# Shared expert of a post-norm transformer block in blocks of 512 tokens for its last six of eight, with a PSUM bank for each half of a chunk

## The chip, the cores and the metric

The kernel runs on one core of a Trainium2 chip. The metric is the device time of one execution in microseconds (us). A core has five engines with instruction queues of their own: PE (TensorE, matrix products; its weight loads are listed apart as PEld), DVE (VectorE), ACT (ScalarE), POOL (GpSimd) and SP (SyncE, which here only issues DMAs). They meet through semaphores. Matmul results go to PSUM, eight banks of 128 partitions x 512 fp32 numbers; everything else lives in SBUF.

## What is computed

The input is x, [2, 1024, 512] in fp32, taken as 2048 tokens of 512 numbers. Attention with low-rank updates on q, k, v and o comes first, then a residual and a layer norm; its result is called x1. The second half is a mixture of experts on x1 with a shared expert beside it, a residual and a last layer norm. That half, cut:

```python
xt = x.reshape(T, d)                                  # T = 2048, d = 512
probs = jax.nn.softmax(xt @ Wg, axis=-1)              # E = 8 experts
eidx = jnp.argmax(probs, axis=-1)
gate = jnp.take_along_axis(probs, eidx[:, None], 1)[:, 0]
pos = ...                                             # running count of tokens per expert
keep = pos < C                                        # C = 256 places per expert
flat = jnp.where(keep, eidx * C + pos, E * C)
xd = zeros(E * C, d).at[flat].set(xt, mode='drop').reshape(E, C, d)
h = silu(einsum('ecd,edh->ech', xd, W1)) * einsum('ecd,edh->ech', xd, W3)   # H = 704
oe = einsum('ech,ehd->ecd', h, W2)
out = take(oe, flat) * (gate * keep)
shared = silu(xt @ sw1) * (xt @ sw3) @ sw2
return out + shared
```

## The kernel before

**Precision.** Every fp32 operand of a large matmul is split into a high part, rounded to TensorE's fp32r type, and a low part that holds the rest. A product is three matmuls: high by high, high by low, low by high. So x1 transposed is held twice (`xth`, `xtl`), a weight chunk holds both parts (`w13s`, `w2s`), and so does a hidden activation (`hs`).

**Stages.** Projections, attention, the output projection (`op`, L744) with the first layer norm, the shared expert (first product at 631.76 us), and then the eight experts one after the other. x1 stays in SBUF in two tiles, `x1a` and `x1b`, eight rows of 128 tokens each, with a gate and a token number behind every row.

**The shared expert** (loop at L1121) goes through eight blocks of 256 tokens. The hidden size of 704 is cut into six chunks of 128, of which the last is 64. For each chunk:
- `ffn1` (L881, matmuls at L890): one PSUM bank `h`, its first 256 columns for W1, the others for W3, 12 matmuls of 256 columns each (four slices of d by three products). A matmul has a 128 x 128 weight as its stationary operand and streams `xth` or `xtl` of the 256 tokens. Chunk 5 has W1 and W3 side by side in one stationary operand and takes 12.
- `glu` (L898): silu on ACT into `sl` (L901), product on DVE in PSUM (L902).
- `split_h` (L907): high part of the hidden activation on ACT (L910), low part on DVE (L916); for chunk 5 on half of the partitions, with one more ACT copy.

`shared_out` (L1049) follows for the block before, called after chunk 1 (`pend()`, L1128): for each half of 128 tokens `ffn2` (L919, matmuls at L934) makes 17 matmuls of 512 columns into a bank `y`, with the hidden activation as the stationary operand; DVE adds the residual into `bt`, and SP stores it to `bs_d` in DRAM.

PSUM has three banks `hp` for h, two `tp` for transposes and small products, two `y`. `hs` has eight buffers, and the transposed token blocks have five (`XTB`).

**What runs between.** A table `SCHED` (L84) says after which (block, chunk) the small operations are issued: `p` transposes a block of tokens (`prep_block`, L537; `xpose`, L461), `a` and `b` make router logits for 256 tokens (`logits_a`, L511: eight matmuls of 256 columns; `logits_b`, L525), `q` and `m` finish the first layer norm. `r` steps through the router (L940), a generator with two stops: `r0` runs up to the prefix sum over tokens per expert, `r1` to the prefix sum of the dropped tokens, `r2` to its end, where the slot of every token is known (`slot_i`, L1035), and POOL scatters 16 rows of 128 tokens to `xd_d` in DRAM with indirect DMAs (L1038). `r0` stands at block 3, chunk 3, `r1` at block 3, chunk 5, `r2` at block 4, chunk 1.

TensorE's order is that of the code. For the other engines the framework's scheduler decides the order within the shared expert; in the expert loop it is that of the code for them too.

**What is fetched for the experts.** `w13_load` (L545; its DMA is at L554) loads a 512 KB chunk of an expert's W1 and W3 over rows of x1 in turn, seven places; the scatters of those rows must be through before. It runs `AHEAD` = 5 chunks ahead of use. `w13_split` (L571) makes the high part on ACT (L562) and the low part on DVE; the six splits of expert 0 are issued in the last block. After block 5 SP is told to read `meta` (gates and token numbers, L1142) and the rows of expert 0 (`load_rows`, L1068, DMA at L1072), which wait for all scatters (`reads_xd`, L1057), and four chunks of W2. `prep_expert(0)` (L1075) transposes these rows (`tpe`, L464) after chunk 3 of the last block. The last `shared_out` runs in expert 0, after its chunk 1.

**The experts** (loop at L1152) use the same `ffn1` and `ffn2` with 256 rows each, so 256 columns to a matmul; this part is the same in both kernels but for one call.

Of the kernel before, what the change touches and what calls it, by code (L numbers as in the profile page):

```python
# [9 lines left out]
F32 = mybir.dt.float32  # L10
# [8 lines left out]
P = 128  # L19
# [5 lines left out]
KC = D // P  # L25
# [30 lines left out]
REC = 5  # L56
NRM = 0
K_AT = 6
XTB = 5


ADDS = {
# [16 lines left out]
OPROJ1 = 0  # L79
NRM_DVE = (NU - 3, NU - 2)  # L80
ROOT_LAG, NORM_LAG = 1, 4
HSB = 8
TAIL = (
    "l0 l1 t0 s0 s1 n1 n2 w0 o1 o2 r0 s2 o3 p0 r1 m0 s3 o4 r2 m1 o5 p1 a0 s4 r3 m2 o6 r4 m3 "  # L84
    "s5 o7 r5 m4"
).split()
SCHED = {
# [4 lines left out]
}  # L92
W13 = 5 * 1024 + 512
W2W = 6 * 512
# [4 lines left out]
def kernel(  # L99
# [5 lines left out]
    def f(ap):  # L105
        return ap.bitcast(F32)
# [331 lines left out]
                prep_w(3, load_w(3))  # L438
            xs = xn

    po, rt, xts = {}, {}, {}
    turn3 = cycle(range(4))
    NB = T // 256

# [7 lines left out]
            return one.tile([P, 512], F32, name=nm, tag="one")  # L452
        return po["ps"].tile([P, 512], F32, name=nm, tag=tag, bufs=bufs)

    def new_xt(nm):
        return (
            po['flx'].tile([P, KC, 256], F32R, name=f"xth{nm}", tag="xth", bufs=XTB),
            po['flx'].tile([P, KC, 256], F32R, name=f"xtl{nm}", tag="xtl", bufs=XTB),
        )

    def xpose(xt, half, row, nm):  # L461
        tp = bank(f"tp{nm}_{half}", "tp", 2)
# [72 lines left out]
        )  # L535

    def prep_block(blk):  # L537
        xts[blk] = new_xt(f"s{blk}")
        for hf in range(2):
            i = blk * 2 + hf  # L540
            xpose(xts[blk], hf, x1[i // 8][:, i % 8, 0:D], f"s{blk}")
# [3 lines left out]
    def w13_load(e, c):  # L545
        w = 512 if c == 5 else 1024
        if e < 0:
            raw = po["frw"].tile([P, 2, 512], F32, name=f"w13r{c}", tag="w13r", bufs=RB)
        else:
            n = (e * 6 + c) % 7  # L550
            raw = x1[n // 4][:, n % 4 * 2 : n % 4 * 2 + 2, 0:D]
        raw = raw[:, : w // 512, :]
        src = s13 if e < 0 else w13[e]
        sp.dma_start(  # L554
            out=raw, in_=src[:, c * 1024 : c * 1024 + w].rearrange("p (a b) -> p a b", b=512)
        )
        wraw[e, c] = raw
# [13 lines left out]
    def w13_split(e, c):  # L571
        w13_high(e, c)
        w13_low(e, c)
# [285 lines left out]
    def w2_load(e, c):  # L859
        if e < 0:  # L860
            raw = fr.tile([P, 512], F32, name=f"w2r{c}", tag="bt", bufs=BTB)
        elif e == E - 1:
            n = (E * 6 + c) % 7
            raw = x1[n // 4][:, n % 4 * 2, 0:D]
        else:
            raw = fr.tile([P, 512], F32, name=f"w2r{e}_{c}", tag="w2r", bufs=4)
        src = s2 if e < 0 else w2[e]
        sp.dma_start(out=raw, in_=src[:, c * 512 : c * 512 + 512])
        wraw[e, 6 + c] = raw
# [9 lines left out]
        wchunk[e, 6 + c] = hl  # L879

    def ffn1(e, blk, xt, c):  # L881
        hp = bank(f"h{e}_{blk}_{c}", "hp", 3)
        wt = wchunk[e, c]
        nw = 1 if c == 5 else 2
        for j in range(nw):
            n = 0
            for k in range(KC):
                ws = [wt[:, q, (k * nw + j) * P : (k * nw + j) * P + P] for q in range(2)]
                for lhs, rhs in ((ws[0], xt[0]), (ws[0], xt[1]), (ws[1], xt[0])):
                    pe.matmul(  # L890
                        hp[:, j * 256 : j * 256 + 256], lhs, rhs[:, k, :],
                        start=n == 0, stop=n == 11,
                    )
                    n += 1
        return hp


    def glu(e, blk, c, hp):  # L898
        sl = fr.tile([P, 256], F32, name=f"sl{e}_{blk}_{c}", tag="sl", bufs=2)
        if c < 5:  # L900
            act.activation(sl, hp[:, 0:256], AF.Silu)  # L901
            dve.tensor_tensor(hp[:, 256:512], hp[:, 256:512], sl, ALU.mult)  # L902
        else:
            act.activation(sl[64:128], hp[0:64, 0:256], AF.Silu)
            dve.tensor_tensor(hp[64:128, 0:256], hp[64:128, 0:256], sl[64:128], ALU.mult)

    def split_h(e, blk, c, hp):  # L907
        hs = fr.tile([P, 2, 256], F32R, name=f"hs{e}_{blk}_{c}", tag="hs", bufs=HSB)
        if c < 5:
            act.copy(hs[:, 0, :], hp[:, 256:512])  # L910
            dve.tensor_tensor(hs[:, 1, :], hp[:, 256:512], f(hs[:, 0, :]), ALU.subtract)
        else:
            pr = hp[64:128, 0:256]
            act.copy(hs[64:128, 1, :], pr)
            act.copy(hs[0:64, 0, :], pr)
            dve.tensor_tensor(hs[64:128, 0, :], pr, f(hs[64:128, 1, :]), ALU.subtract)  # L916
        return hs
# [128 lines left out]
            tc.add_to_no_dep_group("xd", sc_)  # L1046
            scatters.append(sc_)

    def shared_out(blk, hss):  # L1049
        for hf in range(2):  # L1050
            i = blk * 2 + hf
            o = ffn2(-1, blk, hss, hf)
            bt = fr.tile([P, D], F32, name=f"bt{i}", tag="bt", bufs=BTB)
            dve.tensor_tensor(bt, o, x1[i // 8][:, i % 8, 0:D], ALU.add)
            sp.dma_start(out=bs_d[i * P : i * P + P, :], in_=bt)
# [17 lines left out]
            xrows[e, hf] = xd  # L1073

    def prep_expert(e):  # L1075
        xte[e] = new_xt(f"e{e}")
        for hf in range(2):
            xpose(xte[e], hf, xrows[e, hf], f"e{e}")

# [38 lines left out]
    for at, ops in SCHED.items():  # L1118
        sched[at] = [(stage[op[0]], int(op[1])) for op in ops.split()]
    pend = None  # L1120
    for st in range(NB):  # L1121
        hss = []
        for c in range(6):
            hp = ffn1(-1, st, xts[st], c)
            glu(-1, st, c, hp)
            hss.append(split_h(-1, st, c, hp))
            if c == 1 and pend:
                pend()  # L1128
            for fn, a_ in sched.get((st, c), ()):
                fn(a_)  # L1130
            n = (st - NB + 1) * 6 + c
            if 0 <= n + AHEAD < E * 6:
                w13_load(*divmod(n + AHEAD, 6))
            if st == NB - 1:
                if c == 0:
                    load_rows(1)
                if c == 3:
                    prep_expert(0)
                w13_split(0, c)
        if st == NB - 3:  # L1140
            reads_xd(
                sp.dma_start(  # L1142
                    out=meta, in_=xd_d[:, D : D + 2].rearrange("(j p) c -> p j c", p=P)
                )
            )
            load_rows(0)
            for q in range(4):
                w2_load(0, q)
        pend = lambda st=st, hss=hss: shared_out(st, hss)

    with tc.manual_schedule(engines=MAN4):
        last = None  # L1152
        for e in range(E):
            nxt = e + 1
            hss = []
            for c in range(6):
# [13 lines left out]
                if nxt < E:  # L1170
                    if c == 0 and nxt + 1 < E:
                        load_rows(nxt + 1)
                    w13_high(nxt, c)
                hss.append(split_h(e, 0, c, hp))
                if nxt < E:
                    w13_low(nxt, c)
                if c == 1:
                    if e:
                        for hf in range(2):
                            expert_out(e - 1, last, hf)  # L1180
                    else:
                        pend()
                if c == 3 and nxt < E:
                    prep_expert(nxt)
                if e in (0, E - 1) and c in (3, 5):
# [90 lines left out]
```

## Time and profile before

| | |
|---|---|
| median of 10 runs | 1061.19 us (1060.38 to 1063.26) |
| the profiled execution's own time | 1059.73 us |
| its span in the profile | 1058.0 us |
| PE busy | 1034.0 us, 98% |
| DVE, ACT, POOL busy | 686.9, 527.2, 573.5 us |
| the eight experts' FFN1 matmuls (L890, 256 columns), mean of one | 704 of 283 ns and 352 of 285 ns |
| FFN2 matmuls (L934, 512 columns) from `hs`, mean of one | 260 of 390 ns |
| bytes moved by DMA | 151.93 MB, mean 144 GB/s |

The profile is that of one execution, taken by the hardware; its span runs from the first instruction to the last, and the execution's own time has 1.73 us more around it. The page gives, for each engine, busy time and instructions; the span in 40 equal slices (26.45 us each) with the busy share of each engine in tenths, the clock that TensorE was granted (PEclk), and what the DMA engines moved; and groups of equal instructions, each with its line in the code, its output and input, and the mean time of one. Matmuls overlap, so the time of one is longer than the distance from one start to the next. The timeline lists single instructions with their start; in brackets stands how long the engine was idle before and what ended that ("issue": nothing that the profile shows; "remote": a semaphore from elsewhere). A table by windows gives busy time per engine in a chosen stretch.

### The profile page before, as it was taken

What the parts mean: (1) busy time and instruction counts of PE and PEld (TensorE: products, weight loads), DVE (VectorE), ACT (ScalarE), POOL (GpSimd) and SP (SyncE); (2) the same over time, 40 slices, a digit from 0 to 9 for tenths busy, and PEclk for the clock granted to TensorE, in tenths of its full rate; (3) what the DMA queues carried; (4) which work ended last, traced back from release to release, by engine and by line L of the source; (5) the groups of instructions that cost most, each with busy time, mean ns of one, the idle gap of its engine ahead of it and who ended that gap; (6) DMA issues with size and microseconds to landing.
All of it is one profiled execution on the core that took longest, in us unless ns stands there. A gap on an engine that the chain in (4) does not pass through costs nothing. (4 is left out here: it accounts for less than half of the span.)

```text
span 1058.0 us, 16557 instructions
## 1 busy us (share of the span) xinstructions
PE 1034.0 (98%) x5994; PEld 745.2 (70%) x5994; DVE 686.9 (65%) x1192; ACT 527.2 (50%) x1023; POOL 573.5 (54%) x406
## 2 busy tenths in 40 slices
PE   9999999999999999999999999999979999999995
PEld 7888774444444455544444389999969999999994
DVE  7732788788888877778887873324412557777752
ACT  5422216666666645566666635223112447555552
POOL 4000006999999986979995263000320046766674
PEclk9999999999999999999999999999989999999998
DMA  8866863464646553635649441000370456777721
GB/s 293 284 219 213 254 195 91 91 136 109 134 94 147 121 115 83 138 82 125 146 103 188 92 120 52 20 21 20 119 221 31 130 179 228 254 246 243 258 86 59
DMA packets 86025, 151.93 MB, mean 144 GB/s; under 512 B 15492, under 2 KB 24196, under 8 KB 85944
## 3 DMA queue, kind: packets, MB, share of 16 engines
q1 hardware_dynamic: 76344, 117.31, 37.8%
q0 software_dynamic: 9600, 33.58, 13.4%
q8 instruction: 47, 0.77, 0.3%
q14 instruction: 34, 0.28, 0.1%
HBM read 95.83 MB, written 33.78 MB: 123 GB/s over the span
## 5 line engine op out<-in xcount | busy, mean ns | idle before, releaser
L197 DVE TENSOR_REDUCE mt<-s 128x1 f32<-128x512 f32 x512 | 324.0, 682 | 79.0 <-PE s L189 78.6
L659 POOL TENSOR_TENSOR pt<-pt,pt 128x1024 f32<-128x1024 f32 x138 | 336.7, 2943 | 0.1
L629 ACT ACTIVATE pt<-st 128x512 f32<-128x512 f32 x512 | 269.1, 601 | 131.5 <-PE st L620 111.6
L620 PE MATMUL st<-qs,ks 98*128 98x512 f32 x512 | 213.1, 427 | 1.3 <-DVE x1a L347 0.7
L189 PE MATMUL s<-ks,qs 96*128 96x512 f32 x512 | 200.1, 398 | 1.0 <-DVE mt L197 1.0
L620 PEld LDWEIGHTS st<-qs,ks 98*128 98x128 f32 x512 | 95.6, 188 | 133.2 <-issue 93.1
L656 POOL DMA_DIRECT2D pt<-pt x40 | 37.3, 1122 | 187.0 <-PE st L620 163.9
L890 PE MATMUL h<-xthe,w13s 128*128 128x256 f32 x704 | 129.9, 283 | 0.0
L878 POOL TENSOR_TENSOR w2s<-w2r,w2s 128x512 fp32r<-128x512 f32 x42 | 65.9, 1590 | 104.8 <-ACT w2s L877 104.6
L189 PEld LDWEIGHTS s<-ks,qs 96*128 96x128 f32 x512 | 97.0, 189 | 20.4 <-DVE mt L197 5.7
L890 PEld LDWEIGHTS h<-xthe,w13s 128*128 128x128 f32 x704 | 110.7, 191 | 0.3
L890 PE MATMUL h<-xtle,w13s 128*128 128x256 f32 x352 | 100.2, 285 | 0.1
L639 PE MATMUL av<-pt,vt 128*32 128x512 f32 x512 | 75.3, 605 | 0.0
L639 PE MATMUL av<-pt,x1b 128*32 128x512 f32 x512 | 68.2, 605 | 0.0
L890 PEld LDWEIGHTS h<-xtle,w13s 128*128 128x128 f32 x352 | 67.4, 191 | 1.0 <-DVE xtle L468 0.3
L1038 POOL DMA_INDIRECT xd_d<-x1a,slot_i x8 | 7.9, 987 | 110.5 <-DVE slot_i L1035 108.3
L934 PE MATMUL y<-w2s,hs 128*128 128x512 f32 x260 | 60.9, 390 | 0.0
L934 PEld LDWEIGHTS y<-w2s,hs 128*128 128x128 f32 x260 | 48.2, 188 | 10.2 <-DVE hs L916 0.5
L331 ACT ACTIVATE oh<-o,bqk_sb 128x512 fp32r<-128x512 f32 x32 | 22.0, 689 | 57.9 <-PE o L316 54.6
L901 ACT ACTIVATE sl<-h 128x256 f32<-128x256 f32 x40 | 15.5, 386 | 60.4 <-PE h L890 59.1
L316 PE MATMUL o<-xh,wh 128*128 128x512 f32 x116 | 45.3, 391 | 0.1
L316 PE MATMUL o<-xl,wh 128*128 128x512 f32 x116 | 45.3, 390 | 0.0
(830 smaller groups left out, 1842.4 us busy)
## 6 DMA issues: line engine op xcount, KB each, us to landing
pt<-pt POOLq DMA_DIRECT2D x40, 512.0 KB
x1a<-in_w_dram SPq DMA_DIRECT2D x24, 512.0 KB
w2r<-in_w_dram SPq DMA_DIRECT2D x42, 256.0 KB
qkd<-oh SPq DMA_DIRECT2D x32, 256.0 KB
qkd<-ol SPq DMA_DIRECT2D x32, 256.0 KB
x1b<-in_w_dram SPq DMA_DIRECT2D x16, 512.0 KB
qs<-qkd SPq DMA_DIRECT2D x30, 256.0 KB
ks<-qkd SPq DMA_DIRECT2D x18, 256.0 KB
```

The lines of the kernel that those rows point to most:

```text
L189: pe.matmul(s1, Qs[u % 3][0:96, h, qt * P : qt * P + P], Ks[g % 2][0:96, h, kh * 512 : kh * 512 + 512], start=True, stop=True,)
L197: dve.tensor_reduce(mts[u][:, c, kh : kh + 1], s1, AX.X, ALU.max)
L316: pe.matmul(o, lhs, rhs, start=k + i == 0, stop=k + i == KC + 1)
L331: act.activation(oh, o, AF.Identity, bias=bias)
L620: pe.matmul(sb, Ks[g % 2][:, h, kc * P : kc * P + P], Qs[u % 3][:, h, :], start=True, stop=True,)
L629: act.activation(pts[t, h // 2][:, h % 2, :], sb, AF.Exp, scale=SCALE)
L639: pe.matmul(avs[u][32 * h : 32 * h + 32, :], vts[g][:, kc, 32 * h : 32 * h + 32], pts[t, h // 2][:, h % 2, :], start=kc == 0, stop=kc == 7 ...
L656: pool.dma_start(out=pts[i + 1, pr], in_=pts[i, pr], accum_op=ALU.add)
L659: eng.tensor_tensor(accs[u, pr], accs[u, pr], pts[i, pr], ALU.add)
L878: pool.tensor_tensor(hl[:, 1, :], raw, f(hl[:, 0, :]), ALU.subtract)
L890: pe.matmul(hp[:, j * 256 : j * 256 + 256], lhs, rhs[:, k, :], start=n == 0, stop=n == 11,)
L934: pe.matmul(o, lhs, rhs, start=n == 0, stop=n == 16)
```

## The change

The eight blocks of 256 tokens become five: two of 256, then three of 512 (`BLOCKS`, pairs of first block and size). A wide block makes a chunk in two banks, one for W1 and one for W3, with 12 matmuls of 512 columns each (`ffn1_wide`), and the silu, product and split on 512 columns at once (`glu_wide`, `split_wide`). `hp` gets four banks. The transposed tokens lie in pairs of blocks, two buffers of 512 for five of 256; the hidden activations lie in pairs too, four buffers, and the first two chunks of a wide block in the buffers of the raw shared weights.

The four FFN2 halves of a wide block are issued after chunk 0 of the block behind it, and those of the last one in expert 0 after its first chunk. The table of small operations is new: `r0` after chunk 3 and `r1` after chunk 5 of the second wide block, `r2` after chunk 0 of the last one. The reads of `meta`, of expert 0's rows and the four W2 loads stand behind `r2` there. Loads and splits of expert 0's weights go by the same count of chunks, two for each wide one. Raw weights use six places in x1 instead of seven.

```diff
--- before.py
+++ after.py
...
 REC = 5
 NRM = 0
 K_AT = 6
-XTB = 5
+XTB = 2
 
 
 ADDS = {
...
 OPROJ1 = 0
 NRM_DVE = (NU - 3, NU - 2)
 ROOT_LAG, NORM_LAG = 1, 4
-HSB = 8
+HSB = 4
+
+BLOCKS = ((0, 1), (1, 1), (2, 2), (4, 2), (6, 2))
...
 SCHED = {
     (0, 0): "q6 m5", (0, 1): "p2 q7 m6", (0, 2): "a1 m7", (0, 3): "b0", (0, 4): "p3", (0, 5): "b1",
-    (1, 0): "a2 p4", (1, 1): "a3", (1, 2): "b2 a4", (1, 3): "b3 p5", (1, 4): "b4",
-    (1, 5): "p6", (2, 0): "a5", (2, 1): "b5 a6", (2, 3): "b6", (2, 5): "p7",
-    (3, 1): "a7", (3, 2): "b7", (3, 3): "r0", (3, 5): "r1", (4, 1): "r2",
+    (1, 0): "a2", (1, 1): "b2", (1, 2): "a3", (1, 3): "b3",
+    (2, 0): "p4", (2, 1): "a4 p5", (2, 2): "a5", (2, 3): "b4", (2, 4): "b5",
+    (3, 0): "p6", (3, 1): "a6 p7", (3, 2): "b6 a7", (3, 3): "b7 r0", (3, 5): "r1", (4, 0): "r2",
 }
 W13 = 5 * 1024 + 512
 W2W = 6 * 512
...
                 prep_w(3, load_w(3))
             xs = xn
 
-    po, rt, xts = {}, {}, {}
+    po, rt, xts, xts2 = {}, {}, {}, {}
     turn3 = cycle(range(4))
     NB = T // 256
 
...
             return one.tile([P, 512], F32, name=nm, tag="one")
         return po["ps"].tile([P, 512], F32, name=nm, tag=tag, bufs=bufs)
 
-    def new_xt(nm):
-        return (
-            po['flx'].tile([P, KC, 256], F32R, name=f"xth{nm}", tag="xth", bufs=XTB),
-            po['flx'].tile([P, KC, 256], F32R, name=f"xtl{nm}", tag="xtl", bufs=XTB),
-        )
+    pairs = {}
+
+
+    def new_xt(nm, i):
+        if i % 2 == 0:
+            pairs[nm] = [
+                po["flx"].tile([P, KC, 512], F32R, name=f"xt{q}{nm}{i}", tag=f"xt{q}", bufs=XTB)
+                for q in "hl"
+            ]
+        return [z[:, :, i % 2 * 256 : i % 2 * 256 + 256] for z in pairs[nm]]
 
     def xpose(xt, half, row, nm):
         tp = bank(f"tp{nm}_{half}", "tp", 2)
...
         )
 
     def prep_block(blk):
-        xts[blk] = new_xt(f"s{blk}")
+        xts[blk] = new_xt("s", blk)
+        if blk % 2:
+            xts2[blk - 1] = pairs["s"]
         for hf in range(2):
             i = blk * 2 + hf
             xpose(xts[blk], hf, x1[i // 8][:, i % 8, 0:D], f"s{blk}")
...
         if e < 0:
             raw = po["frw"].tile([P, 2, 512], F32, name=f"w13r{c}", tag="w13r", bufs=RB)
         else:
-            n = (e * 6 + c) % 7
+            n = (e * 6 + c) % 6
             raw = x1[n // 4][:, n % 4 * 2 : n % 4 * 2 + 2, 0:D]
         raw = raw[:, : w // 512, :]
         src = s13 if e < 0 else w13[e]
...
         wchunk[e, 6 + c] = hl
 
     def ffn1(e, blk, xt, c):
-        hp = bank(f"h{e}_{blk}_{c}", "hp", 3)
+        hp = bank(f"h{e}_{blk}_{c}", "hp", 4)
         wt = wchunk[e, c]
         nw = 1 if c == 5 else 2
         for j in range(nw):
...
         return hp
 
 
+    def ffn1_wide(blk, xt, c):
+        wt = wchunk[-1, c]
+        hps = []
+        for j in range(1 if c == 5 else 2):
+            hp = bank(f"h{blk}_{c}{j}", "hp", 4)
+            n, nw = 0, 1 if c == 5 else 2
+            for k in range(KC):
+                ws = [wt[:, q, (k * nw + j) * P : (k * nw + j) * P + P] for q in range(2)]
+                for lhs, rhs in ((ws[0], xt[0]), (ws[0], xt[1]), (ws[1], xt[0])):
+                    pe.matmul(hp, lhs, rhs[:, k, :], start=n == 0, stop=n == 11)
+                    n += 1
+            hps.append(hp)
+        return hps
+
+    def glu_wide(blk, c, hps):
+        sl = fr.tile([P, 512], F32, name=f"sl{blk}_{c}", tag="sl", bufs=2)
+        if c < 5:
+            act.activation(sl, hps[0], AF.Silu)
+            dve.tensor_tensor(hps[1], hps[1], sl, ALU.mult)
+        else:
+            act.activation(sl[64:128], hps[0][0:64], AF.Silu)
+            dve.tensor_tensor(hps[0][64:128], hps[0][64:128], sl[64:128], ALU.mult)
+
+
+    def split_wide(blk, c, hps):
+        if c < 2:
+            hs = po["frw"].tile([P, 2, 512], F32R, name=f"hw{blk}_{c}", tag="w13r", bufs=RB)
+        else:
+            hs = fr.tile([P, 2, 512], F32R, name=f"hw{blk}_{c}", tag="hw", bufs=HSB)
+        if c < 5:
+            act.copy(hs[:, 0, :], hps[1])
+            dve.tensor_tensor(hs[:, 1, :], hps[1], f(hs[:, 0, :]), ALU.subtract)
+        else:
+            pr = hps[0][64:128]
+            act.copy(hs[64:128, 1, :], pr)
+            act.copy(hs[0:64, 0, :], pr)
+            dve.tensor_tensor(hs[64:128, 0, :], pr, f(hs[64:128, 1, :]), ALU.subtract)
+        return hs
+
+
     def glu(e, blk, c, hp):
-        sl = fr.tile([P, 256], F32, name=f"sl{e}_{blk}_{c}", tag="sl", bufs=2)
+        sl = fr.tile([P, 512], F32, name=f"sl{e}_{blk}_{c}", tag="sl", bufs=2)[:, 0:256]
         if c < 5:
             act.activation(sl, hp[:, 0:256], AF.Silu)
             dve.tensor_tensor(hp[:, 256:512], hp[:, 256:512], sl, ALU.mult)
...
             tc.add_to_no_dep_group("xd", sc_)
             scatters.append(sc_)
 
-    def shared_out(blk, hss):
-        for hf in range(2):
+    def shared_out(blk, hss, n=2):
+        for hf in range(n):
             i = blk * 2 + hf
             o = ffn2(-1, blk, hss, hf)
             bt = fr.tile([P, D], F32, name=f"bt{i}", tag="bt", bufs=BTB)
...
             xrows[e, hf] = xd
 
     def prep_expert(e):
-        xte[e] = new_xt(f"e{e}")
+        xte[e] = new_xt("e", e)
         for hf in range(2):
             xpose(xte[e], hf, xrows[e, hf], f"e{e}")
 
...
     for at, ops in SCHED.items():
         sched[at] = [(stage[op[0]], int(op[1])) for op in ops.split()]
     pend = None
-    for st in range(NB):
+    for st, (blk, nb) in enumerate(BLOCKS):
         hss = []
         for c in range(6):
-            hp = ffn1(-1, st, xts[st], c)
-            glu(-1, st, c, hp)
-            hss.append(split_h(-1, st, c, hp))
-            if c == 1 and pend:
-                pend()
+            if nb == 1:
+                hp = ffn1(-1, blk, xts[blk], c)
+                glu(-1, blk, c, hp)
+                hss.append(split_h(-1, blk, c, hp))
+            else:
+                hps = ffn1_wide(blk, xts2[blk], c)
+                glu_wide(blk, c, hps)
             for fn, a_ in sched.get((st, c), ()):
                 fn(a_)
-            n = (st - NB + 1) * 6 + c
-            if 0 <= n + AHEAD < E * 6:
-                w13_load(*divmod(n + AHEAD, 6))
-            if st == NB - 1:
-                if c == 0:
-                    load_rows(1)
-                if c == 3:
-                    prep_expert(0)
-                w13_split(0, c)
-        if st == NB - 3:
-            reads_xd(
-                sp.dma_start(
-                    out=meta, in_=xd_d[:, D : D + 2].rearrange("(j p) c -> p j c", p=P)
+            if c == 0 and blk + nb == NB:
+                reads_xd(
+                    sp.dma_start(
+                        out=meta, in_=xd_d[:, D : D + 2].rearrange("(j p) c -> p j c", p=P)
+                    )
                 )
-            )
-            load_rows(0)
-            for q in range(4):
-                w2_load(0, q)
-        pend = lambda st=st, hss=hss: shared_out(st, hss)
+                load_rows(0)
+                for q in range(4):
+                    w2_load(0, q)
+            if c == 2 - nb and pend:
+                pend()
+            if nb == 2:
+                hss.append(split_wide(blk, c, hps))
+            for v in range(c * nb, c * nb + nb):
+                bv, cv = blk + v // 6, v % 6
+                n = (bv - NB + 1) * 6 + cv
+                if 0 <= n + AHEAD < E * 6:
+                    w13_load(*divmod(n + AHEAD, 6))
+                if bv == NB - 1:
+                    if cv == 0:
+                        load_rows(1)
+                    if cv == 3:
+                        prep_expert(0)
+                    w13_split(0, cv)
+        pend = lambda blk=blk, nb=nb, hss=hss: shared_out(blk, hss, 2 * nb)
 
     with tc.manual_schedule(engines=MAN4):
         last = None
...
                     if c == 0 and nxt + 1 < E:
                         load_rows(nxt + 1)
                     w13_high(nxt, c)
+                if e == 0 and c == 0:
+                    pend()
                 hss.append(split_h(e, 0, c, hp))
                 if nxt < E:
                     w13_low(nxt, c)
-                if c == 1:
-                    if e:
-                        for hf in range(2):
-                            expert_out(e - 1, last, hf)
-                    else:
-                        pend()
+                if c == 1 and e:
+                    for hf in range(2):
+                        expert_out(e - 1, last, hf)
                 if c == 3 and nxt < E:
                     prep_expert(nxt)
                 if e in (0, E - 1) and c in (3, 5):
```

Left out: the same change of 7 to 6 in `w2_load`, and in `glu` and `split_h` the cutting of the narrow block's tile out of a 512-wide one (`sl`, `hw`).

More of the change, by code (lines that the diff above doesn't have):

```diff
@@ L862, in w2_load @@
         elif e == E - 1:
-            n = (E * 6 + c) % 7
+            n = (E * 6 + c) % 6
             raw = x1[n // 4][:, n % 4 * 2, 0:D]
@@ L907, in split_h @@
     def split_h(e, blk, c, hp):
-        hs = fr.tile([P, 2, 256], F32R, name=f"hs{e}_{blk}_{c}", tag="hs", bufs=HSB)
+        if c % 2 == 0:
+            pairs["h"] = fr.tile([P, 2, 512], F32R, name=f"hs{e}_{blk}_{c}", tag="hw", bufs=HSB)
+        hs = pairs["h"][:, :, c % 2 * 256 : c % 2 * 256 + 256]
         if c < 5:
```

## The prediction, made before the changed kernel was run

> **What bounds the kernel now.** I read the page's busy list first, then the slices, then the pitch of the matmuls in the timeline, and last the one stretch in which TensorE isn't full.
>
> ```profile
> PE 1034.0 (98%) x5994; PEld 745.2 (70%) x5994; DVE 686.9 (65%) x1192; ACT 527.2 (50%) x1023; POOL 573.5 (54%) x406
> ...
> PE   9999999999999999999999999999979999999995
> ...
> PEclk9999999999999999999999999999989999999998
> ```
>
> TensorE is busy for 98% of the span and in every slice but one and the last; no other engine passes 65%. So the time goes with TensorE's work, and with the one dip in slice 30, where its granted clock dips too. The change works in the shared expert (631.76 to about 842.7 us), which holds that dip.
>
> The 283 and 390 ns that the page gives for a 256-wide and a 512-wide matmul are latencies of overlapping instructions. The price is the pitch, from start to start:
>
> ```profile
> 699.41 0.28 PE L890 MATMUL h-1_2_2_7228<-xths,w13s-1_2_6332 128*128 128x256 f32 x1
> ...
> 702.29 0.28 PE L890 MATMUL h-1_2_3_7259<-xths,w13s-1_3_6376 128*128 128x256 f32 x1
> ...
> 693.99 0.39 PE L934 MATMUL y-1_1_1_7192<-w2s-1_0_6527,hs-1_1_0_6816 128*128 128x512 f32 x1
> ...
> 697.39 0.39 PE L934 MATMUL y-1_1_1_7192<-w2s-1_5_6552,hs-1_1_5_7078 128*128 128x512 f32 x1
> ```
>
> The first pair is one chunk of FFN1 (first product), 24 matmuls: 2.88 us, 0.120 each, so 0.240 for 512 columns. The second pair is 15 matmuls of FFN2 (second product): 3.40 us, 0.2267 each. One wide costs 0.0133 less than two narrow ones.
>
> The dip, by windows (after the length: busy PE, PE loads, DVE, ACT, POOL, then granted clock, share of the DMA engines, GB/s):
>
> ```profile
> 757.00:759.00 2.00, 2.00 (x19) 2.00 (x18) 0.86 (x2) 0.40 (x2) 1.70 (x2) 1.00 0.64 251
> 761.00:763.00 2.00, 2.00 (x19) 2.00 (x19) 1.05 (x3) 1.08 (x3) 1.60 (x2) 1.00 0.98 207
> 767.00:769.00 2.00, 1.27 (x6) 0.76 (x5) 0.00 (x0) 0.00 (x0) 1.69 (x2) 1.00 0.97 376
> 771.00:773.00 2.00, 0.82 (x3) 0.19 (x1) 0.69 (x2) 0.37 (x1) 1.70 (x2) 0.74 1.00 390
> 773.00:775.00 2.00, 0.63 (x2) 0.57 (x2) 0.00 (x0) 0.00 (x0) 1.39 (x3) 0.50 1.01 268
> 777.00:779.00 2.00, 1.41 (x4) 1.02 (x4) 0.28 (x1) 0.38 (x1) 0.00 (x0) 0.50 0.68 261
> 779.00:781.00 2.00, 2.00 (x6) 1.53 (x5) 1.23 (x3) 0.37 (x1) 0.00 (x0) 0.50 0.02 6
> ```
>
> From 755.40 POOL issues 16 scatters of tokens (L1038), one each 1.27 us until 774.61. Alone they leave TensorE full (757 to 759). From 760.48 four 512 KB loads of expert 0's weights, each released by two scatters, fill the DMA engines. Some 5 us later TensorE starves, with no wait that the profile names ("issue" in the timeline), and ACT sees TensorE's ends late:
>
> ```profile
> 772.46 0.58 PE L934 MATMUL y-1_4_0_7974<-w2s-1_2_6537,hs-1_4_2_7827 128*128 128x512 f32 x1 [1.18 <-issue]
> ...
> 778.31 0.38 ACT L901 ACTIVATE sl-1_5_1_7968<-h-1_5_1_7943 128x256 f32<-128x256 f32 x1 [6.63 <-remote]
> ```
>
> When the share falls to 0.02 TensorE is full again, at half clock until 782.2. The two FFN2 halves there took 767.00 to 784.81, 17.81 us, against 7.72 for the same pair elsewhere (660.04 to 667.76): 10.1 lost, with 0.4 just before it 10.5. I call it the jam.
>
> **The change, part by part.** *Wide FFN1.* 792 narrow matmuls of blocks 2 to 7 become 396 wide ones, in three blocks of 132. At the FFN2 pitch this saves 396 x 0.0133 = 5.2 us. FFN2 is the right row because its stationary size, moving width and accumulation are those of the new matmuls; the slowest 512-wide row, the o projection (L744, 612.21 to 616.90, 20 matmuls, 0.2345), would leave 396 x 0.0055 = 2.2. So 5.2, bounds 2.2 and 5.2; TensorE bounds the stage, so it counts in full.
>
> [...] The measured pitches differ by 13.3 ns, and I go by these.
>
> *Vector work.* One silu, multiply, cast and subtraction on 512 columns replace two on 256. Narrow rows: ACT 386 and 375 ns, DVE 428 and 425. Wide rows elsewhere: ACT 0.60 (L629), DVE 0.68. A wide chunk's chain is thus 0.60 + 0.68 + 0.60 + 0.68 = 2.6 us, about 3.3 with 0.2 for each hand-over. A bank is needed again two chunks later, 2 x 24 x 0.2267 = 10.9 us. Cost 0, hidden by TensorE with 7 us of room; an ACT that is told 6.6 late, as above, would use that up. The hidden activations of the block before are 15 us old when FFN2 reads them. ACT and DVE lose some 40 instructions each; nothing waits for them.
>
> *FFN2 in fours.* Four halves (15.4 us) run after chunk 0 instead of two after chunk 1; the same number of matmuls. The last four move into expert 0 behind its first chunk. Order only: 0.
>
> *Router, logits, transposes.* They issue the same instructions. The router's two DVE chains (pio 736.7 to drop 742.0; pid 750.2 to the slots at 755.1, some 5 us each) lie under TensorE. In the last one, the slots' transposes on TensorE come behind chunk 0 of the last wide block (its start: S), the scatters at about S + 10.5. A TensorE wait for the first chain is 0 to 0.3. POOL keeps its order.
>
> *The jam, moved.* In before it lay two blocks ahead of the last; now the same 16 scatters lie in the last block. Its makers remain: the same 19.2 us of scatters, and loads released by pairs of them. SP now issues chunk loads 0 to 5 among them, six against four, interleaved with the four stores of FFN2's halves, and a seventh (waiting for ACT's split of chunk 0) ahead of the rows. Nothing else in the change lightens it. The three more loads are 1.31 MB (one has only 256 KB), at 0.29 to 0.39 MB/us 3.4 to 4.5 us of full DMA, in which TensorE gets about half (windows 767 to 775: 0.63 to 1.27 of 2.00): +2.0. On the other side the loads may be spaced by the stores; that is a guess, and I put it at -0.5. I take a jam of 12, +1.5. Bounds: 4, where only a wait for expert 0's rows is left (next paragraph), and 20, the old loss stretched by seven loads over four (10.5 x 7/4 = 18.4) and a second ACT delay.
>
> *What comes next.* Expert 0's rows were read 5.1 us after the last scatter landed (779.94 to 785.1) and used only here:
>
> ```profile
> 837.67 0.38 PE L464 MATMUL tpe<-ident,xd 128*128 128x128 f32 x2
> ```
>
> That is 53 us of cover, and it is gone. Now: scatters at S + 10.5, landed 24.5 later as in before, S + 35; rows 5.1 later, S + 40; behind 2 MB of further loads and stores in the queues (at 0.3 MB/us, 6 to 7 us) S + 46 to 47. TensorE reaches these transposes after five chunks and the four halves, at S + 43.05 if nothing stalls: a wait of 3 to 4, but none if the jam of 12 has already made TensorE late. So the two aren't added; the floor of the jam is 4. The weights: ACT's split of load k stands between the silu and the cast of chunk k, so a late load holds a bank of FFN1. By the old lags after the first scatter (9.4, 12.8, 17.8, 22.0) loads 0 to 3 land at S + 20 to 32.5, and TensorE wants chunk 0's, 1's and 2's banks again at S + 26, 32 and 37: after split, cast and subtraction (1.0 + 0.6 + 0.7) 4 us or more to spare, cost 0, and what comes later than that is paid in full.
>
> *Six raw slots instead of seven.* A load starts one chunk later, 4.2 us; six chunks of lead remain in the expert phase, where the DMA moves 230 to 258 GB/s and TensorE is full. 0; a missed load would cost up to one 512 KB transfer, 2 us, at each expert.
>
> Sum, on the profiled execution's 1059.73 (span 1058.0): -5.2 + 1.5 = -3.7, 1056.0. That run is 1.46 below the median of ten, 1061.19, so on the median 1057.5. With a jam of length L the median is 1061.19 - 15.7 + L.
>
> **Rivals.** *The jam shrinks.* Matmuls of FFN1 ran full for 5 us at a share of 0.98, and if the stores hold the loads back, FFN2 escapes. L of 4 to 8: 1049.5 to 1053.5. For: fewer instructions for the same work. Against: the same scatters and more bytes.
>
> *Eaten up.* The pitch is that of the o projection (-2.2), or the jam takes 13.5 to 17.7: 1059.1 to 1063.2. For: two to three more loads in the jam. Against: the dip of before began some 6 us after the DMA filled, and the first loads lie later in the scatter train only if stores hold them.
>
> *Slower: expert 0 waits behind the scatters.* The place is the transposes of expert 0's rows and the splits of its weights in ACT's queue. In before 53 us lay between; now the rows must come within 43 us + jam of S. From L = 17.7 the gain is gone: that is, rows at S + 61 or later, or ACT, stuck on a late load, holding a bank of FFN1. With L of 18 to 22: 1063.5 to 1067.5; I put it at 1065. For: SP issues the meta and row reads behind seven loads and behind stores that wait for TensorE itself, so the jam feeds its own delay. Against: on the old lags the rows are there at S + 47.
>
> *It doesn't do what it says*, the wide blocks running at the pitch of two narrow ones: 1063 with the jam of 12, inside "eaten up".
>
> **How the numbers follow.** A measurement of this kernel can tell about 0.2% (2.1 us): faster is below 1059.07, slower above 1063.31. Forecast, jam within 8 to 13.5 at the full pitch, 1053.5 to 1059: 0.47. Jam shrinks: 0.15. Eaten up: 0.18. Slower: 0.20. Faster is 0.62, same 0.18, slower 0.20. The range leaves out about a tenth at each end: half of the shrinking case below 1050, half of the slower one above 1065.5. The likeliest sign's own range is 1050 to 1059.
>
> **What would show it.** Wide FFN1: 24 matmuls of a wide chunk in 5.44 us (0.2267); at 0.2345 they take 5.63. The jam: one stretch with a granted clock of 0.50 and DMA share near 1.0, beginning some 10 us after the first scatter, now in the last wide block, next to h or y of that block; if no window there has TensorE under 1.9 of 2.00, the shrinking case holds. The rows: a wait of the transposes at L464 for the row DMA of over 1 us shows the cover gone. ACT waiting for a load in its weight splits, followed by TensorE waiting for ACT, shows the slower case. I am wrong above all if the jam isn't made by scatters and loads together, or if it grows with its bytes faster than I assume.

## The result, and the profile after

The changed kernel takes 1049.19 us in the median of 9 runs (1047.12 to 1051.9), the one before 1061.42 (31 runs): a ratio of 0.9887, interval 0.9876 to 0.9897, or about 12 us less. Forecast were 1057.5 and a range from 1050. The profiled execution took 1048.33 us. Its page, in the lines that answer to those shown of before:

```profile
span 1046.6 us, 15667 instructions
...
PE 1026.2 (98%) x5598; PEld 720.8 (69%) x5598; DVE 678.3 (65%) x1156; ACT 520.8 (50%) x984; POOL 574.7 (55%) x406
...
PE   8999999999999999999999999999999999999995
...
PEclk9999999999999999999999999999999999999998
DMA  9876873464646563355656722000108657777731
```

There are 396 matmuls fewer, and the dip of slice 30 is gone from both rows. To see where the time went I added up the distances from each matmul's start to the next one's, by kind, from the first product of the shared expert to the first FFN2 matmul of expert 0 (631.76 to 873.13 in before, 633.11 to 861.94 after):

| us | before | changed | difference |
|---|---|---|---|
| shared FFN1 | 129.19 | 124.70 | -4.49 |
| shared FFN2 | 71.98 | 62.67 | -9.31 |
| token transposes | 5.34 | 5.87 | +0.53 |
| logits and prefix sums | 11.52 | 11.55 | +0.03 |
| expert 0's FFN1 and transposes | 23.33 | 24.03 | +0.70 |
| the stretch | 241.37 | 228.83 | -12.54 |

What follows the stretch is the same (184.90 and 184.69), and what lies ahead of it differs by 1.35 us, within the spread of the runs below that leave that part alone (631.2 to 633.4). The pitch came nearly as worked out; the larger part is the jam. The scatters start at 785.44 now and are issued until 805.51. Windows of the changed kernel (columns as before):

```profile
796.00:798.00 2.00, 2.00 (x10) 1.63 (x9) 0.00 (x0) 1.00 (x2) 1.70 (x2) 1.00 1.04 405
...
804.00:806.00 2.00, 2.00 (x11) 1.65 (x10) 0.00 (x0) 0.00 (x0) 1.45 (x2) 1.00 1.12 366
806.00:808.00 2.00, 1.60 (x7) 1.00 (x6) 0.00 (x0) 0.60 (x1) 0.47 (x1) 1.00 1.04 197
808.00:810.00 2.00, 1.92 (x9) 1.58 (x9) 1.44 (x2) 1.82 (x3) 0.00 (x0) 1.00 0.96 333
```

For 10 us the DMA engines are as full as in the old jam, among the same scatters, and TensorE is full at full clock. Only at 807 does it miss 0.8 us (the six steps from 806.40 to 808.55 take 2.15 instead of 1.36). The timeline of TensorE from the start of the last wide block, around 807, through the next chunk, and at the point where rows were expected late:

```profile
775.20 0.48 PE L916 MATMUL h<-xths,w13s-1_0_6235 128*128 128x512 f32 x1
...
808.08 0.39 PE L916 MATMUL h<-xtls,w13s-1_2_6332 128*128 128x512 f32 x1 [0.48 <-issue]
...
808.55 0.39 PE L916 MATMUL h<-xths,w13s-1_3_6376 128*128 128x512 f32 x1
...
814.01 0.39 PE L916 MATMUL h<-xths,w13s-1_4_6449 128*128 128x512 f32 x1
...
819.46 1.03 PE L471 MATMUL tpe<-ident,xd 128*128 128x128 f32 x8
...
823.82 0.38 PE L899 MATMUL h<-xtle,w13s 128*128 128x256 f32 x1 [0.45 <-DVE xtle L475]
```

The transposes of expert 0's rows wait for nothing, 44.3 us after the start of the last wide block (775.20). What is late is the low part of the transposed rows, by 0.45 us.

### The profile page after: what moved, and what is told of

Same layout as the page of the kernel before. It is cut to its first block, busy times and chain, and to the rows that moved or that the text cites. A ratio compares the mean times of both kernels' runs of the same rounds, so it can differ in the third digit from the quotient of the medians.

```text
span 1046.6 us, 15667 instructions
## 1 busy us (share of the span) xinstructions
PE 1026.2 (98%) x5598; PEld 720.8 (69%) x5598; DVE 678.3 (65%) x1156; ACT 520.8 (50%) x984; POOL 574.7 (55%) x406
## 3 DMA queue, kind: packets, MB, share of 16 engines
q0 software_dynamic: 9600, 33.58, 13.6%
## 5 line engine op out<-in xcount | busy, mean ns | idle before, releaser
L577 DVE TENSOR_TENSOR w13s<-x1a,w13s 128x1024 fp32r<-128x1024 f32 x32 | 47.3, 1477 | 4.9 <-issue 4.2
```

Source lines behind the costliest of these rows:

```text
L577: (pool if e < 0 else dve).tensor_tensor(lo, raw, f(hi), ALU.subtract)
```

## Experiments: what starves TensorE

My theory on record was *saturation*: scatters and loads together fill the DMA engines. Its rival after seeing the result: TensorE's *code*. The trace shows a DMA packet of 16384 B on a queue of its own for about every 256 TensorE instructions (47 packets in before for 5994 matmuls and as many weight loads), and in before one fell due just where the jam begins, as estimated from the pitch: 128 matmuls of 0.120 us after the packet at 751.11 end at 766.5 (the next packet came at 773.10). How much of its code TensorE holds no run here shows. A third: *wide* matmuls can't be starved. (Starved means here that TensorE has work and no wait that the profile names, and still starts its matmuls late; a train is the 16 scatters one behind the other.)

**e1**, loads held until the scatters are through:

```diff
-        sp.dma_start(
+        ld = sp.dma_start(
...
+        if e == 0 and c < 4:
+            reads_xd(ld)
```

> The kernel before, but expert 0's first four weight loads wait for all 16 scatters, so that they no longer run among them. Saturation theory (scatters and loads together fill the DMA engines and starve TensorE): no jam, y of block 4 back at 7.72 us, about -10.5 us against before (1051). Code-fetch theory (TensorE's next 16 KB of instructions falls due while the DMA engines are full): no jam either, since nothing fills them then. Scatters alone as the cause: the jam stays, 1061.

Measured: 0.9989 (0.9975 to 1.0004), no gain. Windows of e1, whose first load is issued at 784.98:

```profile
764.00:766.00 2.00, 2.00 (x19) 2.00 (x18) 0.47 (x2) 1.11 (x3) 1.46 (x2) 1.00 0.57 218
...
770.00:772.00 2.00, 0.75 (x4) 0.55 (x4) 0.00 (x0) 0.00 (x0) 1.70 (x2) 0.97 0.66 255
...
774.00:776.00 2.00, 1.17 (x3) 0.40 (x2) 0.00 (x0) 0.00 (x0) 1.57 (x2) 0.50 0.64 243
```

TensorE starves with a third of the DMA engines' time or more free. The saturation theory has fallen; it takes no loads: from 757.01 to 779 the scatters are the only DMAs that the program issues.

**e2**, 32 tiny fp32 matmuls (64 in the records) in the start:

```diff
+PAD = 32
...
             warm("hot", WARM)
+            pad = one.tile([P, 512], F32, name="pad", tag="one")
+            for i in range(PAD):
+                pe.matmul(pad[:, 0:8], bo_bc[:, 0:P], bo_bc[:, 0:8], start=True, stop=True)
```

> The kernel before with 32 tiny extra matmuls on TensorE in its idle start, some 128 more TensorE instructions ahead of everything, so that each 16 KB piece of its code falls due half a piece (about 7.7 us) earlier; all else as before. Saturation theory: nothing changes, the jam begins some 11 us after the first scatter (766.4 in before) and costs 10.5 us: 1061. Code-fetch theory: the piece that fell due at 766.4 now does so near 758.7, ahead of the full DMA engines, and the next near 774: the jam at 766 is gone, a shorter one may start at 774; 1051 to 1056.

Measured: 1.0108 (1.0079 to 1.0136); the start wasn't idle, and the first shared product comes 10.3 us later (642.08), which is nearly all of the loss. The jam begins 9.6 us after the first scatter and 5.6 us after a code packet that came in good time. The code theory has fallen too. How TensorE starves there (timeline of e2):

```profile
777.24 0.37 PE L894 MATMUL h-1_5_1_7976<-xtls,w13s-1_1_6273 128*128 128x256 f32 x1 [0.44 <-issue]
778.65 0.28 PE L894 MATMUL h-1_5_1_7976<-xths,w13s-1_1_6273 128*128 128x256 f32 x1 [1.04 <-issue]
780.05 0.37 PE L894 MATMUL h-1_5_1_7976<-xths,w13s-1_1_6273 128*128 128x256 f32 x1 [1.12 <-issue]
```

Matmuls start 1.4 us apart (0.70 and 0.71 between some): one instruction, weight load or matmul, in about 0.7 us.

**e3**, the scatters later:

```diff
-    (3, 1): "a7", (3, 2): "b7", (3, 3): "r0", (3, 5): "r1", (4, 1): "r2",
+    (3, 1): "a7", (3, 2): "b7", (3, 3): "r0", (3, 5): "r1", (4, 4): "r2",
```

> The kernel before with the router's last part after chunk 4 instead of chunk 1 of block 4, so that scatters and loads come some 8.7 us later against TensorE's work. Saturation theory: the same jam of about 10 us, starting 11 us after the first scatter, now in chunks 2 and 3 of block 5 instead of the second product: 1061. Code-fetch theory: no jam at 11 us after the first scatter but from the next piece on, about 16 us after the 766 of before, near 782, where the scatters end: a jam of 0 to 5 us, 1051 to 1056. If only the second product can be starved: little or no jam.

Measured: 0.9975 (0.9960 to 0.9991). The jam begins 14.2 us after the first scatter, in FFN1, and is 8.6 us long: none of the three accounts fits.

**e4**, the changed kernel with blocks 6 and 7 narrow:

```diff
-BLOCKS = ((0, 1), (1, 1), (2, 2), (4, 2), (6, 2))
+BLOCKS = ((0, 1), (1, 1), (2, 2), (4, 2), (6, 1), (7, 1))
...
-    (3, 0): "p6", (3, 1): "a6 p7", (3, 2): "b6 a7", (3, 3): "b7 r0", (3, 5): "r1", (4, 0): "r2",
+    (3, 0): "p6", (3, 1): "a6 p7", (3, 2): "b6 a7", (3, 3): "b7 r0", (3, 5): "r1", (4, 1): "r2",
...
-            if c == 0 and blk + nb == NB:
+            if c == 1 and st == 4:
```

> The changed kernel with its last wide block taken as two narrow ones again (blocks 6 and 7 of 256 tokens, FFN2 of blocks 4 and 5 after chunk 1 of block 6), two wide blocks left. The pitch alone: one third of the gain from it given back, +1.6 us. If wide matmuls are what keeps TensorE from starving (half as many instructions per us), a jam of some 10 us is back in block 6 or 7: about 1061. Saturation theory has no account of why the changed kernel had none; by the stores among the loads, still none: 1051. Code-fetch theory: a piece lasts 15 us in narrow blocks instead of 28, so one falls due in the full stretch: a jam of up to 10 us.

Measured: 0.9939 (0.9917 to 0.9962), half of the gain, with a jam of 7.8 us that begins 15.0 us after the first scatter. Windows of e4:

```profile
798.00:800.00 2.00, 2.00 (x19) 1.95 (x17) 0.00 (x0) 0.00 (x0) 1.70 (x2) 1.00 1.04 406
800.00:802.00 2.00, 0.34 (x2) 0.33 (x2) 0.62 (x1) 0.00 (x0) 1.39 (x3) 1.00 1.00 230
```

The onset in time is 10, 14, 15 or 22 us, but counted in TensorE's own work it is nearly fixed. The table has every run so far, all with an unbroken train (starved: the next matmul comes over 0.49 us later):

| run | first scatter to first starved matmul, us | matmuls started between | last scatter's issue to the end, us |
|---|---|---|---|
| before | 10.7 | 89 | 3.5 |
| e1 | 10.8 | 84 | 3.7 |
| e2 | 9.6 | 80 | 3.7 |
| e3 | 14.2 | 87 | 3.6 |
| e4 | 15.0 | 79 | 3.6 |
| changed | 21.8 | 94 | 2.6 |

The new theory, *supply*: while POOL's scatters run TensorE lives on a stock of some 75 to 95 matmuls with their weight loads, and is filled up again only about 3.6 us (2.6 in the changed kernel) behind the last scatter's issue. FFN1 in narrow matmuls (0.120) uses the stock up in 10 us, wide ones (0.2267) in 21; the train with its tail lasts 23. The next runs test that.

**e5**, a pause after every fourth scatter until it has landed:

```diff
+        slot_g = slot_i
         for i in range(NT):
+            if i and i % 4 == 0:
+                slot_g = fl.tile([P, NT], I32, name=f"slot{i}")
+                cp = pool.tensor_copy(slot_g[:, i : i + 4], slot_i[:, i : i + 4])
+                tc.add_manual_dep(
+                    cp.ins, scatters[-1].name,
+                    mybir.DependencyInfo(mybir.DependencyClass.Sync, mybir.DependencyReason.DATA),
+                    reason="pause",
+                )
             sc_ = pool.indirect_dma_start(
                 out=xd_d,
-                out_offset=bass.IndirectOffsetOnAxis(ap=slot_i[:, i : i + 1], axis=0),
+                out_offset=bass.IndirectOffsetOnAxis(ap=slot_g[:, i : i + 1], axis=0),
```

> The kernel before with a pause after every fourth scatter: POOL waits until it has landed before it issues the next four. Supply theory (while POOL issues scatters TensorE lives on a stock of some 80 to 90 matmuls and gets one or two instructions per 0.7 us after that, until about 3.6 us behind the last scatter; a pause lets it fill up again): no group of four lasts long enough (4 x 1.27 us), no jam, -10 us, 1051. If the stock is only filled behind all 16, or the jam goes with the number or bytes of scatters: it begins after the same 80 to 90 matmuls and lasts longer, 1061 or more.

Measured: 0.9884 (0.9868 to 0.9901): narrow blocks, the old order, and the whole gain of the change. No matmul starves; POOL and windows of e5:

```profile
760.83 0.96 POOL L1047 DMA_INDIRECT xd_d<-x1a,slot_i  x1 [0.30 <-issue]
764.29 0.19 POOL L1041 COPY slot<-slot_i 128x4 int32<-128x4 int32 x1 [2.50 <-DMA xd_d<-x1a,slot_i]
765.29 0.98 POOL L1047 DMA_INDIRECT xd_d<-x1a,slot  x1 [0.81 <-POOL slot L1041]
```

```profile
774.00:776.00 2.00, 2.00 (x12) 1.70 (x11) 0.19 (x1) 0.00 (x0) 1.43 (x2) 1.00 0.93 256
778.00:780.00 2.00, 2.00 (x19) 2.00 (x18) 0.37 (x1) 0.39 (x1) 0.27 (x1) 1.00 1.00 390
```

**e6 and e7**, 16 more row blocks written to a buffer that nobody reads, after the last logits, by POOL's indirect DMA or by SP's plain one:

```diff
+    def extra(_):
...
+            ex_ = pool.indirect_dma_start(
+                out=xe_d,
+                out_offset=bass.IndirectOffsetOnAxis(ap=tok2[:, i : i + 1], axis=0),
+                in_=x1[i // 8][:, i % 8, 0:D],
...
+            ex_ = sp.dma_start(out=xe_d[i * P : i * P + P, :], in_=x1[i // 8][:, i % 8, 0:D])
```

> The kernel before with 16 more scatters of the same rows by POOL to a buffer that nobody reads, issued after the logits of the last block, some 27 us ahead of the real ones, where no load runs. Supply theory: a second jam there, starting after 80 to 90 matmuls and ending 3.6 us after the last extra scatter, and the old one as well: +8 to +11 us, about 1071. If it takes expert loads or the place in the code: no second jam, 1061 to 1062.

> The same 16 row blocks of 256 KB written to the same buffer at the same place, but as plain DMAs from SP instead of indirect ones from POOL. Supply theory with POOL's indirect DMAs as the cause: no second jam, 1061 to 1062, though the same bytes move faster. If bytes or full DMA engines starve TensorE: a second jam, 1066 to 1071.

Measured: e6 1.0157 (1.0140 to 1.0174), e7 1.0015 (1.0000 to 1.0030). In e6 there are two jams, after 77 and 75 matmuls, ending 3.6 and 3.8 us behind the last issue; they are 13.6 and 13.8 us long, against 12.0 in before, and the loss of some 16.5 us is more than I expected. First line: e6, in the extra train; below, e7, while SP moves the same bytes:

```profile
746.00:748.00 2.00, 0.37 (x1) 0.29 (x1) 1.54 (x9) 0.00 (x0) 1.39 (x3) 0.50 0.43 162
```

```profile
732.00:734.00 2.00, 2.00 (x19) 2.00 (x18) 0.52 (x3) 1.67 (x2) 0.00 (x0) 1.00 1.04 384
738.00:740.00 2.00, 2.00 (x19) 2.00 (x19) 1.80 (x9) 0.31 (x2) 0.00 (x0) 1.00 1.03 385
```

Here full DMA engines (1.04 and 1.03) leave TensorE full (2.00 of 2.00), a train of POOL's scatters at a share of 0.43 doesn't (0.37). SP's rows are through about 12 us after the first issue, while e6 begins to starve 9.2 us after its own, so e7 outlasts that point by some 3 us only, with twice the bytes moved by then (3.2 MB against 1.6). For longer stretches speaks the page of the changed kernel: in slices 34 to 38, among the experts, mostly SP's loads keep the DMA engines at 0.7 for 130 us, and TensorE is full. The two runs differ in two things, the engine that issues and the indirection; which of them matters, no run separates. (e7's own jam, at the real train, starts after 79 matmuls and ends 4.2 us behind the last issue; it is 13.9 us long, about as much longer as e7 loses, 1.6 us.)

**e9**, e5 without the wait for the landing, so that only the copy lies between the fours:

```diff
-                    mybir.DependencyInfo(mybir.DependencyClass.Sync, mybir.DependencyReason.DATA),
+                    mybir.DependencyInfo(
+                        mybir.DependencyClass.NoSync, mybir.DependencyReason.SCHED_ONLY
+                    ),
```

> The kernel before with one tiny POOL copy after every fourth scatter, without waiting for these to land: the train is broken only by about 1 us each time and lasts some 23 us instead of 19. If any gap in POOL's issuing lets TensorE's stock fill up: no jam, 1049 to 1051, as with the long pauses. If it fills only when the scatters have been worked off (about 3.6 us behind the last one issued): the jam is there as in before, or longer by the 3 us of the copies, 1061 to 1064.

Measured: 0.9986 (0.9975 to 0.9996), the jam as before (after 83 matmuls). POOL of e9, and a window of its jam:

```profile
759.44 0.96 POOL L1049 DMA_INDIRECT xd_d<-x1a,slot_i  x1 [0.30 <-issue]
760.40 0.20 POOL L1041 COPY slot<-slot_i 128x4 int32<-128x4 int32 x1
760.87 0.98 POOL L1049 DMA_INDIRECT xd_d<-x1a,slot  x1 [0.28 <-issue]
```

```profile
766.00:768.00 2.00, 0.94 (x5) 0.53 (x4) 0.00 (x0) 0.00 (x0) 1.57 (x2) 1.00 0.94 343
```

The copy fits into the gap that was there; the scatters come 1.43 us apart there instead of 1.27. So POOL doing something else for 0.2 us doesn't fill the stock; the pauses of e5 do, in which 4.4 to 6.2 us lie between the starts of two scatters. Whether the landing does it or the time without a new scatter, e5 and e9 don't separate, but the traces of three other runs speak for the time: TensorE is full again while packets of the scatters are still to come, until 812.94 in the changed kernel (full from 808.08), 811.48 in e4 (from 807.74) and 789.50 in e3 (from 786.93). A pause of 4 us that doesn't wait for the landing was not run.

**Better versions.** e8 makes blocks 0 and 1 wide too, with the small operations packed into half as many slots:

```diff
-BLOCKS = ((0, 1), (1, 1), (2, 2), (4, 2), (6, 2))
+BLOCKS = ((0, 2), (2, 2), (4, 2), (6, 2))
...
+    (0, 0): "q6 m5 p2 q7 m6", (0, 1): "a1 m7 b0", (0, 2): "p3 b1", (0, 3): "a2", (0, 4): "b2 a3",
+    (0, 5): "b3",
...
```

> The changed kernel with blocks 0 and 1 wide too, four blocks of 512 tokens. By the pitch measured in the changed kernel (4.75 us for three blocks) -1.6 us, if the small operations still fit and the weights of the shared expert are split in time; 0 to -1.6. Against before: 1047.5 to 1049.5 on before's 1061.4.

Measured: 0.9872 (0.9855 to 0.9888), 1047.55 us. FFN1 falls to 123.38 us, but the transposes rise to 7.08, and there is a starved stretch of 2.2 us (from 20.5 us after the first scatter, 89 matmuls). The last three keep e8's four wide blocks. e10 and e11 add one pause after the eighth scatter (e9's and e5's edit with 8 for 4); e12 has e5's pause and moves the last four FFN2 halves and the transposes ahead of expert 0's first chunk:

```diff
-                    if cv == 3:
-                        prep_expert(0)
...
+                if e == 0 and c == 0:
+                    pend()
+                    prep_expert(0)
                 hp = ffn1(e, 0, xte[e], c)
...
-                if e == 0 and c == 0:
-                    pend()
```

> Four wide blocks, with one tiny POOL copy after the eighth scatter (about 1 us). If a short gap fills TensorE's stock: the 2.2 us of starved matmuls that the four wide blocks still had at the end of the train are gone, rows about 1 us later, 1045.5 to 1047 on before's 1061.3. If not: as without the copy or up to 1 us worse, 1047.5 to 1048.5.

> Four wide blocks, with POOL waiting after the eighth scatter until it has landed (about 3.5 to 5 us). The starvation at the end of the train is gone in either theory (-2 us), but expert 0's rows come 3.5 to 5 us later, and they had some 2 us to spare at their transposes: a wait of 1 to 4 us there. Sum -1 to +2 us against four wide blocks without it: 1046.5 to 1049.5.

> Four wide blocks, the scatters in fours with each four landed before the next, and the last four FFN2 halves (15.6 us) ahead of expert 0's row transposes instead of behind its first chunk, so that the rows have time. Supply theory: no starved stretch (-2.2 us against four wide blocks in the profile), no wait for the rows at the transposes, and the 0.7 us that expert 0's first chunk lost for its transposed low part stays or shrinks. Stage of 225.9 to 227 us against 228.86, a ratio to before of 0.984 to 0.987. If the pauses only move the loss to expert 0's rows or weights: as with four wide blocks, 0.987 to 0.990.

Measured: e10 0.9886 (0.9867 to 0.9906), a starved stretch of 3.9 us after 82 matmuls; e11 0.9874 (0.9859 to 0.9888), nothing starved; e12 0.9882 (0.9864 to 0.9899), nothing starved. What the landed pauses win comes back as a wait; first line e11, below e12:

```profile
818.64 0.63 PE L471 MATMUL tpe<-ident,xd 128*128 128x128 f32 x4 [1.98 <-DMA xd<-xd_d]
```

```profile
837.53 0.38 PE L899 MATMUL h<-xthe,w13s 128*128 128x256 f32 x1 [0.72 <-ACT xthe L474]
838.36 0.39 PE L899 MATMUL h<-xtle,w13s 128*128 128x256 f32 x1 [0.45 <-DVE xtle L475]
```

In e11 the rows are 2 us late; in e12 they are there, and nothing lies between the transposes and their first use. No version is clearly apart from the changed kernel; all intervals overlap its own.

## Why the prediction was wrong

- *Wide FFN1, -5.2* (its own factors, 396 x 0.0133, give 5.3): right. Against e5, whose narrow blocks don't starve, FFN1 falls from 128.69 to 123.9 (124.70 without the 0.8 at 807): -4.8, or 12.1 ns for each of 396 against the 13.3 forecast. The chunk above took 5.46 us (808.55 to 814.01), 24 x 0.2275.
- *The jam, moved: 12, bounds 4 and 20*. This is the step that failed: the term stood at 10.5 + 1.5, and 0.8 was measured. "Nothing else in the change lightens it" was wrong, for the wide matmuls do: the stock is spent in matmuls, so halving their rate nearly outlasts the train (21.8 us of 23). And its makers were named wrongly. The loads among the scatters, which I counted and let lengthen it, aren't needed for it (e1), and full DMA engines don't make it (e7); five of the six counted were issued before the last scatter (792.14 to 803.96). The windows had shown a full share and a starved TensorE side by side, and I took the one for the cause, though the 5 us in which they didn't agree were in the text. "Alone they leave TensorE full (757 to 759)" was read in the first 4 us of the train, before the stock was spent. Nor does the end of the jam go with the DMA share: the changed kernel's TensorE is full again from 808.08 at shares of 0.96 to 1.04.
- *What comes next, a wait of 3 to 4 as the floor*: wrong. The rows were there by S + 44.3 (S, the start of the last wide block, is 775.20) instead of S + 46 to 47: the last scatter's packets ended 3 us later than taken, at S + 37.7, but the rows needed at most 6.5 us from there, not 11 to 12. Only the low part of the transposed rows came 0.45 us late. The floor of the jam fell with it, and so the lower end of the range.
- *Rivals*. "The jam shrinks" came closest (1049.5 to 1053.5), with the right sign for "fewer instructions for the same work", priced too small. "Slower" and "eaten up" had no part in it.
- *Vector work, 7 us of room*: no TensorE wait, but ACT saw the first product of chunk 1 only at 806.71, about 7 us after its last matmul (799.38 to 799.76), and the room was used up. *FFN2 in fours* cost a little: 62.67 against 61.90 in e5. *Transposes*, costed at nothing, took 0.53 more. *Six slots*: no wait, as said.

The stretch adds up: -4.8 for the pitch, -10.6 for the jam of before (FFN1 and FFN2 against e5: 0.5 and 10.1), +0.8 for what is left of it, +0.8, +0.5 and +0.7 for FFN2, transposes and expert 0: -12.6, against the measured -12.54.

## What to carry to other kernels

Where an engine runs dry and the profile names no releaser, count its own instructions from each candidate's start, not only the time: a count that stays nearly fixed while the time doubles points to a stock that is used up. A full resource beside a stall is a coincidence until one of them has been run without the other. In this kernel, POOL's indirect DMAs ran beside TensorE without starving it in groups of four (narrow and wide matmuls) and of eight (wide), each group landed before the next, and larger matmuls kept TensorE running longer beside an unbroken train (94 in 21.8 us, against 89 in 10.7).

## What was not expected of the hardware

- Sixteen indirect DMAs of POOL in a row, at a DMA share of 0.42 to 0.66 (e1), take TensorE down to an instruction in about 0.7 us (e2) after 75 to 94 matmuls; 16 plain ones of SP at a share of 1.0 don't (e7). What the stock consists of stays open: signals from TensorE to ACT are late in the same stretches too (7 us in the changed kernel), so it may be instructions on their way in, or what each finished one has to report.
- The half clock at the jams came in pieces, by the trace's record of the clock: 10.24 us in before (771.98 to 782.22), and 13.65, 6.83 and 3.41 us in other runs (e6 shows 0.50 in every window from 742 to 754), 3, 4, 2 and 1 times 3.413. It didn't come at all after the 0.8 us of starving in the changed kernel, nor after the 2.2 us in e8 (1.00 in its windows up to 808). TensorE wasn't idle throughout ahead of it: in the 3.41 us before the half clock, the length of the shortest piece, it was busy for 1.62 in before and for 1.45 in e11, where the wait for the rows alone brought one piece; in e8 2.42 busy of 3.41 brought none. What starts a piece and what ends it no run here shows.
